# Decoder layer on one core: the norms' small products pinned inside block products, the first context loaded in 8 steps, constant products at the start, the last norm in pairs

## The chip, the cores and the metric

The kernel runs on one core of a Trainium2 chip. The time is device microseconds of one execution. Before the change it is 2510.47 us, the median of 3 runs (2509.59 to 2512.47). One execution was also profiled; all profile rows come from it.

## The reference

The program is one decoder layer in float32: 8 sequences of 100 tokens with 1024 features each, and a context of 722 tokens for each sequence. Three parts follow one another, each with a residual and a layer norm without weights:

```python
def _layernorm(x, axis=-1, eps=1e-05):
    m = jnp.mean(x, axis=axis, keepdims=True)
    v = jnp.var(x, axis=axis, keepdims=True)
    return (x - m) / jnp.sqrt(v + eps)
...
    # retention: 8 heads, keys of 128, values of 256, rotary embedding, decay mask
    scores = jnp.einsum('bihd,bjhd->bhij', q * scale, k) * D[None]
    o = jnp.einsum('bhij,bjhd->bihd', scores, v)
    rms = jax.lax.rsqrt(jnp.mean(o * o, axis=-1, keepdims=True) + EPS)
    o = o * rms * g_norm_weight
    o = o * (g * jax.nn.sigmoid(g))
    return o.reshape(B, T, H * DV) @ Wo
...
    # attention over context and own tokens: 16 query heads, 4 key heads of 128, RMS-normed q and k
    scores = jnp.einsum('blhd,bmhd->bhlm', q, k_full) * scale + mask
    probs = jax.nn.softmax(scores, axis=-1)
    out = jnp.einsum('bhlm,bmhd->blhd', probs, v_full)
    return out.reshape(B, L, NUM_HEADS * HEAD_DIM) @ wo
...
    # feed-forward, 4096 hidden
    return jnp.einsum('bsh,dh->bsd', jax.nn.silu(gate) * up, w_down)
...
x = _layernorm(x + _L0_attn_ref(x, ...))
x = _layernorm(x + _L0_xattn_ref(x, ctx_2048, ...))
x = _layernorm(x + _L0_ffn_ref(x, ...))
```

## The kernel before

Features lie on the 128 partitions, tokens along the free dimension. The 800 tokens are handled in two halves of N = 400 (4 sequences each). A vector of 1024 features is KT = 8 blocks of 128; QT = 4 is half of that.

**Products.** A float32 product is made of three fp32r matmuls: every operand is split in a high part (a cast on ScalarE, L67) and a low part (a subtraction on VectorE, L68), and `mm3` (L86 to L88) adds high x high, high x low and low x high in PSUM. One block product of 128 features over 1024 is `proj`: 8 k steps of 3 matmuls, 24 in all. An output projection (`out_proj`, called for both layer norms of the attention parts) has 2048 inputs, so a block takes 48 matmuls. PSUM has 3 banks under tag `a`, 4 under `s`, 1 under `v`.

**Weights** are loaded by `load_w`: a DMA of 512 KB on SP's queue into one of three `wst` tiles, and the split into one of four `w` tiles. Context tiles (`cs`, in `load_context`) use the same three `wst` tiles.

**Order of the work.** The program is traced in the order in which the code stands. A planner then orders each engine's instructions by priority (trace order) and by its own reckoning of when each is ready. Each engine works its own queue strictly in the planned order. `tc.keep_in_program_order` holds one instruction behind the one traced just before it on the same engine; before the change, only a few instructions are held so.

**Stages.** From the start to 430 us: retention (`w1`), mostly by a scheme of seven products in place of eight (`seven`). To 590 us: output projection and first norm (`out_proj` with `wo1`). To 850 us: queries, own keys and values (`w2`, the loop around L637), each with a rotary embedding (`rope`, L133 to L137), an RMS norm whose sum goes over the partitions on GpSimd (`all_red`, L125), and a store to DRAM (L654). In between lie `load_context(0)` (traced after the first four queries), and two early key products of the context. To 1610 us: attention of each sequence, with its context loaded one sequence at a time. To 1740 us: output projection and second norm (`wo2`). To 2450 us: feed-forward. The end is the last quarter of the down projection and the third norm (L995 to L1023).

**Norms.** The sum over features is a product with a constant matrix of 1/1024 (`onem`; `onem7` has 1/896): an F32 matmul, recorded as two instructions. The first half of each norm is handled by `norm_root`: the mean product (L279) after all eight blocks, 8 subtractions, squares and their sums (L260, L265), a variance product (L283), the inverse root (`inv_root`, L113 to L120), 8 scalings (L271). The second half is split in an early and a late part. `norm_early` takes the mean of the first seven blocks (six in the last norm) at L294, subtracts it (L297) and starts the variance (L299) while the last block is being computed. `norm_more` adds the last block's sum to `delta` (L305) and its squares to the variance (L306). `norm_late` corrects by delta: L312, L313, then 8 subtractions (L316), and scales. `s1` is the running sum of the blocks (L254); y is filled at L239, in the last norm at L1013 and L1014.

After the second norm `after2` (L795) mixes the two halves into the operands of the seven-product scheme.

Of the kernel before, what the change touches and what calls it, by code (L numbers as in the profile page):

```python
# [16 lines left out]
P = 128  # L17
# [17 lines left out]
NEG = -1.0e30  # L35
LN_EXP = "natural_log_exp_and_others"
# [3 lines left out]
def decoder_layer(ctx, tc, xT, cT, w1, wo1, w2, wo2, wc, w3, wd, gw, qw, kw, trig, dec, mask, out):  # L40
# [29 lines left out]
    def load_w(src, w=None, parts=1):  # L70
        st = wp.tile([P, KT * P], F32, tag="wst", name="wst", bufs=3)
        if w is None:
            w = wp.tile([P, 2, KT * P], FR, tag="w", name="w", bufs=4)
        for i in range(parts):
            c = slice(i * KT * P // parts, (i + 1) * KT * P // parts)
            nc.sync.dma_start(out=st[:, c], in_=src[:, c])
            split(w[:, :, c], st[:, c])
        return w
# [6 lines left out]
    def mm3(acc, lh, ll, rh, rl, start, stop, chain=False):  # L85
        nc.tensor.matmul(acc, lh, rh, start=start, stop=False, skip_group_check=chain)  # L86
        nc.tensor.matmul(acc, lh, rl, start=False, stop=False, skip_group_check=chain)  # L87
        nc.tensor.matmul(acc, ll, rh, start=False, stop=stop, skip_group_check=chain)  # L88

    def mmw(acc, w, k, rh, rl, start, stop):  # L90
        c = slice(k * P, (k + 1) * P)
        mm3(acc, w[:, 0, c], w[:, 1, c], rh, rl, start, stop)
# [7 lines left out]
    def proj(w, z, n=N, tag="a"):  # L100
        acc = bank(tag)[:, :n]
        for k in range(KT):
            t = z[k // QT]
            mmw(acc, w, k, t[:, 0, k % QT, :n], t[:, 1, k % QT, :n], k == 0, k == KT - 1)
        return acc
# [69 lines left out]

    def const(v, name):
        t = cp.tile([P, 1], F32, name=name)
        nc.vector.memset(t, v)
        return t
# [36 lines left out]
    def out_proj(half, w, load_o, res, yp, ybufs, p, make_z, dst, after=None):  # L216

        og = load_o(half)
        y = yp.tile([P, KT, N], F32, tag="y", name="y", bufs=ybufs)
        s1 = p.tile([P, N], F32, tag="s1", name="s1", bufs=2)  # L220
        first = 4 if half == 0 else 1
        for ms in [range(first)] + [[m] for m in range(first, KT)]:
            if half == 1 and KT - 1 in ms:
                early = norm_early(y, s1, p)
            accs = [bank(("aaasaaaa", "sssaaass")[half][m])[:, :N] for m in ms]
            for c in range(2):
                for m, acc in zip(ms, accs):
                    wt = load_w(w[m, c])
                    for k in range(KT):
                        kt = c * KT + k  # L230
                        rh, rl = og(kt)
                        a = acc if len(rh.shape) == 2 else bt(acc)
                        mmw(a, wt, k, rh, rl, kt == 0, kt == 2 * KT - 1)
            for m, acc in zip(ms, accs):
                rs = yp.tile([P, N], F32, tag="rs", name="rs", bufs=2)
                nc.sync.dma_start(out=rs, in_=res[half, :, m])
                if half == 1 and m == KT - 1:
                    nc.vector.tensor_tensor(rs, rs, early[0], ALU.subtract)
                nc.vector.tensor_tensor(y[:, m], acc, rs, ALU.add)  # L239
                if half == 0 or m < KT - 1:  # L240
                    add_up(s1, y, m)
        z = make_z(half)
        if half == 0:
            scaled(y, norm_root(y, s1, p), lambda m: dst[half, :, m], z)
        else:
            norm_more(y, early, p, KT - 1)
            norm_late(y, early, p, lambda m: dst[half, :, m], z)
        if after is not None:
            after(half, y)
        return z  # L250
# [25 lines left out]
    def norm_root(y, s1, p):  # L276
        n = y.shape[2]
        mean = bank("s")[:, :n]
        nc.tensor.matmul(mean, onem, s1, start=True, stop=True)  # L279
# [11 lines left out]
    def norm_early(y, s1, p, first=KT - 1):  # L291
        n = y.shape[2]
        mean = bank("s")[:, :n]
        nc.tensor.matmul(mean, onem7, s1, start=True, stop=True)  # L294
        f = (KT - 1) / first
        for m in range(first):
            nc.vector.scalar_tensor_tensor(y[:, m], mean, -f, y[:, m], ALU.mult, ALU.add)  # L297
        var, delta = bank("v")[:, :n], bank("s")[:, :n]
        nc.tensor.matmul(var, onem, squares(y, p, range(first)), start=True, stop=False, skip_group_check=True)  # L299
        return mean, var, f, delta, first  # L300

    def norm_more(y, early, p, m):

        _, var, _, delta, first = early
        nc.tensor.matmul(delta, onem, y[:, m], start=m == first, stop=m == KT - 1, skip_group_check=True)  # L305
        nc.tensor.matmul(var, onem, squares(y, p, [m]), start=False, stop=m == KT - 1, skip_group_check=True)  # L306

    def norm_late(y, early, p, dst, z=None):
        _, var, _, delta, _ = early
        n = y.shape[2]  # L310
        vs = p.tile([P, n], F32, tag="vs", name="vs")
        nc.scalar.activation(vs, delta, AF.Square)  # L312
        nc.vector.tensor_tensor(vs, var, vs, ALU.subtract)  # L313
        r = inv_root(p, vs, eps_ln, n)
        for m in range(KT):
            nc.vector.tensor_tensor(y[:, m], y[:, m], delta, ALU.subtract)  # L316
        scaled(y, r, dst, z)
# [104 lines left out]
    with sbuf("l1", 2) as p:  # L422
# [4 lines left out]
        for half in range(2):  # L427
            for j in (1, 2):
                zb["b%d%d" % (j, half + 1)] = big([P, 2, QT, N])
            if half == 0:  # L430
                w0 = load_w(w1[0, 0], parts=4)
            for k in range(KT):
                xs = temp()
                nc.sync.dma_start(out=xs, in_=xT[half, :, k])
# [89 lines left out]

        for i in range(2):
            for half in range(2):
                of_qk(half, i, proj((w0, wk0)[i], x[half]))
            mixed(i)
        for blk in range(2):
            w = load_w(w1[0, 2 + blk])  # L530
            for half in range(2):
                of_v(half, blk, proj(w, x[half]), True)
# [36 lines left out]
    z1p = z1pool.__enter__()  # L569
    with sbuf("ln1", 1) as p:  # L570
        z1 = [out_proj(half, wo1, load_o1, xT, p, 2, p, lambda _: [z1p.tile([P, 2, QT, N], FR, tag="z", name="z")
                                                                 for _ in range(2)], zd) for half in range(2)]
# [6 lines left out]
    def load_context(b):  # L579

        cz.clear()
        for hf in range(2):
            n = SN[hf]
            z = [big([P, 2, QT, SH]) for _ in range(2)]
            for k in range(0, KT, 2):
                cs = wp.tile([P, KT * P], F32, tag="wst", name="cs", bufs=3)
                cs = cs[:, :2 * n].rearrange("p (k n) -> p k n", k=2)
                nc.sync.dma_start(out=cs, in_=cT[b, :, k:k + 2, hf * SH:hf * SH + n])
                split(z[k // QT][:, :, k % QT:k % QT + 2, :n], cs)
            cz.append(z)  # L590
# [31 lines left out]
    early = []  # L622
    with sbuf("l2", 2) as p:
        for kv in range(NKV):
            for i0, i1 in ((0, 4), (4, 6)) if kv == 0 else ((0, 2), (2, 4), (4, 6)):
                if (kv, i0) == (0, 4):
                    load_context(0)
                ws = [load_w(w2[kv, i]) for i in range(i0, i1)]
# [5 lines left out]
                for half in range(2):  # L634
                    bs = slice(half * NB, (half + 1) * NB)
                    for i in range(i0, i1):
                        acc = proj(ws[i - i0], z1[half], tag=acc_tag())  # L637
# [157 lines left out]
    def after2(half, y):  # L795
        if half == 0:
            return
# [17 lines left out]

    with sbuf("lnp2", 1) as p:
        z2 = [out_proj(half, wo2, load_o2, zd, y2p, 1, p, make_z2, zd2, after2) for half in range(2)]
# [10 lines left out]
    ws = [[load_w(w3[i, part]) for part in range(2)] for i in range(2)]  # L828
    gs = {}
    for half in range(2):  # L830
        for i in range(2):
            ag, au = (proj(w, z2[half], tag=acc_tag()) for w in ws[i])
# [153 lines left out]

    for name in C:
# [9 lines left out]
    with sbuf("ln3", 2, "right") as lnp:  # L997
        ws = []
        for half in range(2):
            y = rows(half)  # L1000
            s1 = lnp.tile([P, N], F32, tag="s1", name="s1", bufs=2)
            early = None
            for m in range(KT):
# [5 lines left out]
                elif m == KT - 2:  # L1009
                    early = norm_early(y, s1, lnp, m)  # L1010
                acc = proj(ws[m], z3[half], tag=acc_tag())
                if early:
# [82 lines left out]
```

## Time and profile before

| | |
|---|---|
| median of the runs | 2510.47 us |
| profiled execution | 2510.48 us |
| its span, from first to last instruction | 2508.7 us |
| TensorE busy | 2461.3 us (98%) |
| VectorE busy | 1994.6 us (80%) |
| ScalarE busy | 1343.3 us (54%) |
| GpSimd busy | 478.8 us (19%) |
| mean DMA rate over the span | 173 GB/s |
| mean granted TensorE clock | 0.996 |

Times in rows are in us from the start of the span; a name such as L86 is the line of the kernel, and `a<-big,w` names the tile written and those read. Matmuls overlap at their ends, so the distance from one start to the next tells their pace: 0.18 us for 400 columns at full clock.

### The profile page before, as it was taken

How to read it: one execution, taken by the hardware profiler on the slowest of the kernel's cores; microseconds unless marked ns; L12 is line 12 of the kernel's file. 1: busy time of each engine (PE TensorE's matmuls, PEld its weight loads, DVE VectorE, ACT ScalarE, POOL GpSimd, SP SyncE). 2: the span in 40 equal slices, each digit the busy share in tenths (PEclk: the TensorE clock that was granted, in tenths of full speed). 3: DMA queues.
4: the chain of work that ended last, by engine and by line, in shares of the span. 5: the costliest groups of instructions: out<-in, count | busy, mean ns of one | idle time of the engine just before them, and what ended most of it. 6: DMA issues, size and time to landing. Idle time of an engine off the chain costs nothing.

```text
span 2508.7 us, 37154 instructions
## 1 busy us (share of the span) xinstructions
PE 2461.3 (98%) x14036; PEld 2438.4 (97%) x14036; DVE 1994.6 (80%) x3110; ACT 1343.3 (54%) x2264; POOL 478.8 (19%) x234
## 2 busy tenths in 40 slices
PE   8999999999899999999999999999999999999997
PEld 8999999999899999999999999999999999999997
DVE  7678877568999798999989998866987777666756
ACT  6667676335767565566666666533544444432221
POOL 0111111002555334433433434100000000000000
PEclk9999999999999999999999999999999999999999
DMA  7334445774444654554554563675455444389731
GB/s 241 111 111 127 137 142 185 237 270 146 150 148 132 213 175 143 173 173 142 168 186 133 174 195 116 209 253 162 137 178 196 166 169 162 121 297 329 259 100 53
DMA packets 224450, 433.96 MB, mean 173 GB/s; under 512 B 47338, under 2 KB 168042, under 8 KB 211854
## 3 DMA queue, kind: packets, MB, share of 16 engines
q1 hardware_dynamic: 223118, 427.39, 50.9%
q0 software_dynamic: 1152, 4.19, 1.1%
q8 instruction: 110, 1.80, 0.3%
q14 instruction: 70, 0.57, 0.1%
HBM read 322.18 MB, written 109.35 MB: 172 GB/s over the span
## 4 chain that ended last, share of the span: by engine, by line
PE 85%; DVE 9%; ACT 2%; issue 2%; DMA 2%; SPq 0%; DVEq 0%; ACTq 0%
PE a L88 17%; PE a L86 17%; PE a L87 17%; PE s L88 9%; PE s L87 9%; PE s L86 9%; PE v L87 1%; PE v L88 1%; PE v L86 1%; DVE r L120 1%; PE s L491 1%; PE s L688 1%; DVE r L119 1%; DVE w L68 1%; DVE t L650 1%
## 5 line engine op out<-in xcount | busy, mean ns | idle before, releaser
L86 PE MATMUL a<-big,w 128*128 128x400 f32 (+2 forms) x1808 | 610.5, 339 | 10.8 <-ACT big L67 7.3
L87 PE MATMUL a<-big,w 128*128 128x400 f32 (+2 forms) x1808 | 610.5, 338 | 0.0
L88 PE MATMUL a<-big,w 128*128 128x400 f32 (+2 forms) x1808 | 609.2, 338 | 0.0
L67 ACT CAST w<-wst 128x1024 fp32r<-128x1024 f32 (+1 forms) x231 | 239.4, 1038 | 389.9 <-PE a L88 134.9
L68 DVE TENSOR_TENSOR w<-wst,w 128x1024 fp32r<-128x1024 f32 (+1 forms) x231 | 282.9, 1226 | 119.2 <-ACT w L67 118.1
L86 PEld LDWEIGHTS a<-big,w 128*128 128x128 f32 x1808 | 341.1, 189 | 12.2 <-ACT big L67 7.3
L87 PEld LDWEIGHTS a<-big,w 128*128 128x128 f32 x1808 | 341.5, 189 | 1.3 <-DVE big L68 0.3
L88 PEld LDWEIGHTS a<-big,w 128*128 128x128 f32 x1808 | 341.5, 189 | 0.6
L86 PE MATMUL s<-big,w 128*128 128x400 f32 x664 | 230.6, 347 | 0.1
L88 PE MATMUL s<-big,w 128*128 128x400 f32 x664 | 229.0, 346 | 0.4 <-DVE w L68 0.4
L87 PE MATMUL s<-big,w 128*128 128x400 f32 x664 | 229.2, 345 | 0.0
L125 POOL PARTITION_ALL_REDUCE ss<-sq x56 | 160.5, 2871 | 332.9 <-DMA zd<-y 167.1
L605 POOL PARTITION_ALL_REDUCE kss<-ksq x64 | 171.9, 2686 | 121.9 <-ACT ksq L604 121.4
L86 PE MATMUL a<-z,w 128*128 128x400 f32 x488 | 169.6, 348 | 9.2 <-ACT r L118 5.6
L88 PE MATMUL a<-z,w 128*128 128x400 f32 x488 | 170.1, 349 | 0.7 <-DVE w L68 0.7
L87 PE MATMUL a<-z,w 128*128 128x400 f32 x488 | 170.0, 348 | 0.0
L87 PE MATMUL s<-z,w 128*128 128x400 f32 x400 | 138.1, 345 | 2.4 <-DVE z L68 2.4
L86 PE MATMUL s<-z,w 128*128 128x400 f32 x400 | 138.5, 347 | 0.0
L88 PE MATMUL s<-z,w 128*128 128x400 f32 x400 | 138.3, 346 | 0.0
L722 ACT ACTIVATE s<-s,rk 128x400 f32<-128x400 f32 x160 | 87.5, 591 | 90.9 <-DVE sm L742 65.3
L86 PEld LDWEIGHTS s<-big,w 128*128 128x128 f32 x664 | 124.6, 188 | 1.4 <-ACT w L67 0.4
L88 PEld LDWEIGHTS s<-big,w 128*128 128x128 f32 x664 | 125.1, 188 | 0.7 <-DVE w L68 0.7
(330 smaller groups left out, 5642.3 us busy)
## 6 DMA issues: line engine op xcount, KB each, us to landing
wst<-in_w SPq DMA_DIRECT2D x135, 512.0 KB
w<-wcd SPq DMA_DIRECT2D x64, 1024.0 KB
wst<-in_wo SPq DMA_DIRECT2D x64, 512.0 KB
hd<-h SPq DMA_DIRECT2D x12, 1400.0 KB
wst<-in_wd SPq DMA_DIRECT2D x64, 256.0 KB
big<-o1d SPq DMA_DIRECT2D x16, 800.0 KB
qd<-d SPq DMA_DIRECT2D x32, 400.0 KB
q<-qd SPq DMA_DIRECT2D x32, 400.0 KB
```

Of the source, the lines that this page charges most:

```text
L67: nc.scalar.copy(hi, src)
L68: nc.vector.tensor_tensor(lo, src, f32(hi), ALU.subtract)
L86: nc.tensor.matmul(acc, lh, rh, start=start, stop=False, skip_group_check=chain)
L87: nc.tensor.matmul(acc, lh, rl, start=False, stop=False, skip_group_check=chain)
L88: nc.tensor.matmul(acc, ll, rh, start=False, stop=stop, skip_group_check=chain)
L119: nc.vector.scalar_tensor_tensor(q, ss, eps, q, ALU.add, ALU.mult)
L120: nc.vector.scalar_tensor_tensor(q, q, 3.0, r, ALU.subtract, ALU.mult)
L125: nc.gpsimd.partition_all_reduce(y, x, P, op)
L491: nc.tensor.matmul(bt(o)[:, b], vv[:, b * P:(b + 1) * P], pf[:, b], start=True, stop=True)
L605: nc.gpsimd.partition_all_reduce(ss[:, at], sq[:, at], P, RED.add)
L650: nc.vector.scalar_tensor_tensor(t, t, -0.5 if i < 4 else -0.5 * math.sqrt(P), r, ALU.mult, ALU.mult)
L722: nc.scalar.activation(sc, sp, AF.Copy, scale=rk[:, c:c + 1])
```

## The change

Six things change.

1. `proj` and `out_proj` take a table `todo` of work to be traced ahead of a given k step. The products of a norm (mean, delta, variance) are traced and pinned there, inside the next block product: the means ahead of k step 4; delta ahead of step 4 and the variance ahead of step 7 of the first projection of the following stage. So the first projection with `w2[0,0]` and with `w3[0,0]` moves ahead of the late part of the norms.
2. The second halves' norm no longer scales the mean (`norm_early` only serves seven blocks), and in `norm_late` the 8 subtractions are pinned in order, 4 ahead of the variance's and 4 behind.
3. The first context is loaded in 8 steps, one after each of 8 projections of the first key head, each with its DMA pinned on SP's queue; before, all 8 were traced at once.
4. Weights for the first four queries, for the V blocks and for the first gate and up products are loaded at other places in the trace order; the very first weight comes by ScalarE's DMA queue and its split alternates with that of x.
5. 22 products of the constant matrix with itself stand at the start.
6. The last norm of the second half is a function of its own, `norm_last`, which subtracts and squares two blocks at a time (128 x 800).

```diff
+WARM = 22
...
+    def mm3(acc, lh, ll, rh, rl, start, stop, chain=False, pinned=False):
+        i = nc.tensor.matmul(acc, lh, rh, start=start, stop=False, skip_group_check=chain)
+        if pinned:
+            pin(i)
...
+    def proj(w, z, n=N, tag="a", todo=None):
         acc = bank(tag)[:, :n]
         for k in range(KT):
+            pinned = between(todo, k)
...
+    warm = bank("v")
+    for _ in range(WARM):
+        nc.tensor.matmul(warm[:, 0:P], onem, onem, start=True, stop=True)
...
             if half == 1 and KT - 1 in ms:
-                early = norm_early(y, s1, p)
-            accs = [bank(("aaasaaaa", "sssaaass")[half][m])[:, :N] for m in ms]
+                todo = {QT: lambda: early.update(norm_early(y, s1, p))}
...
         if half == 0:
-            scaled(y, norm_root(y, s1, p), lambda m: dst[half, :, m], z)
-        else:
-            norm_more(y, early, p, KT - 1)
-            norm_late(y, early, p, lambda m: dst[half, :, m], z)
+            return {QT: whole}, y
+        sq = squares(y, p, [KT - 1])
+        return {QT: lambda: summed(early["delta"], y[:, KT - 1], True, True),
+                KT - 1: lambda: (summed(early["var"], early["sq"], True), summed(early["var"], sq, False, True), late())}, y
+
+    def summed(acc, x, start=False, stop=False):
+
+        pin(nc.tensor.matmul(acc, onem, x, start=start, stop=stop, skip_group_check=True))
...
+        e["vs"] = p.tile([P, N], F32, tag="vs", name="vs")
+        nc.scalar.activation(e["vs"], e["delta"], AF.Square)
+        less(range(QT))
+        pin(nc.vector.tensor_tensor(e["vs"], e["var"], e["vs"], ALU.subtract))
+        less(range(QT, KT))
...
-                w0 = load_w(w1[0, 0], parts=4)
+                for i in range(QT):
+                    c = slice(2 * i * P, 2 * (i + 1) * P)
+                    nc.scalar.dma_start(out=st[:, c], in_=w1[0, 0][:, c])
...
+            wv.append(load_w(w1[0, 2 + i]))
             mixed(i)
         for blk in range(2):
-            w = load_w(w1[0, 2 + blk])
...
+        ws2 = [load_w(w2[0, 0])]
+        acc2 = [proj(ws2[0], z1[0], tag=acc_tag(), todo=todo)]
...
-                nc.sync.dma_start(out=cs, in_=cT[b, :, k:k + 2, hf * SH:hf * SH + n])
+                i = nc.sync.dma_start(out=cs, in_=cT[b, :, k:k + 2, hf * SH:hf * SH + n])
+                if pinned:
+                    pin(i)
...
-                if (kv, i0) == (0, 4):
-                    load_context(0)
...
+                        if kv == 0 and (half == 1 or i0 == 4):
+                            next(ctx0, None)
...
+    def norm_last(y, s1, p, dst):
+        first = KT - 2
+        pair = lambda i: y2[i][:, :, y.at]
+        wide = lambda ap: ap[:, None, :].to_broadcast([P, 2, N])
...
+        prods(0, range(QT))
+        pin(nc.tensor.matmul(mean, onem7, s1, start=True, stop=True))
+        prods(0, range(QT, KT))
+        f = (KT - 1) / first
+        sqs = []
+        for i in range(first // 2):
+            nc.vector.scalar_tensor_tensor(pair(i), wide(mean), -f, pair(i), ALU.mult, ALU.add)
+            sqs.append(p.tile([P, 2, N], F32, tag="sw", name="sw", bufs=3))
+            nc.scalar.activation(sqs[-1], pair(i), AF.Square)
+        pin(nc.vector.tensor_tensor(sqs[0], sqs[0], sqs[1], ALU.add))
+        q6 = add_block(0)
+        pin(nc.vector.tensor_tensor(sqs[0], sqs[0], sqs[2], ALU.add))
+        prods(1, range(KT))
+        q7 = add_block(1)
+        pin(nc.vector.tensor_tensor(sqs[1][:, 0], sqs[0][:, 0], sqs[0][:, 1], ALU.add))
+        summed(delta, y[:, KT - 2], start=True)
+        summed(var, q6, start=True)
+        summed(delta, y[:, KT - 1], stop=True)
+        summed(var, sqs[1][:, 0])
+        summed(var, q7, stop=True)
+        less = lambda i: pin(nc.vector.tensor_tensor(pair(i), pair(i), wide(delta), ALU.subtract))
+        less(0)
+        vs = p.tile([P, N], F32, tag="vs", name="vs")
+        nc.scalar.activation(vs, delta, AF.Square)
+        less(1)
+        pin(nc.vector.tensor_tensor(vs, var, vs, ALU.subtract))
+        less(2)
+        less(3)
+        scaled(y, inv_root(p, vs, eps_ln), dst)
```

## The prediction

> **What bounds the kernel now.** I read the page's head first, then the list of what TensorE waited for, then each engine's busy time in 10 us stretches where those waits lie, then single instructions at the start and the end.
>
> ```profile
> span 2508.7 us, 37154 instructions
> PE 2461.3 (98%) x14036; PEld 2438.4 (97%) x14036; DVE 1994.6 (80%) x3110; ACT 1343.3 (54%) x2264; POOL 478.8 (19%) x234
> ```
>
> TensorE is the bound: 2508.7 - 2461.3 = 47.4 us without a matmul, and of these some 19 us are the tail after the last block product. A change that leaves the products alone can win only from these 47 us and from matmuls run at half clock. Who holds TensorE up:
>
> ```profile
> PE a L86 <- ACT big L67: 7.3, 1, 7.3
> PE a L86 <- ACT r L118: 5.6, 1, 5.6
> PE a L86 <- ACT w L67: 4.2, 5, 1.3
> PE s L279 <- DVE s L254: 2.6, 2, 1.4
> PE s L87 <- DVE z L68: 2.4, 1, 2.4
> ```
>
> The columns are total us, times, longest. The first is the start. L279 is a norm's mean product, which stands directly behind the block product whose result it still has to wait for (at 510.9 us and 1659.2 us). The last is z1 of the second half, late at 605 us. The 5.6 us wait on "ACT r L118" is a PSUM bank not yet read out, at 629 us; what stands behind it shows in the stretches (columns: stretch, length, then busy us and count of PE, PEld, DVE, ACT, POOL):
>
> ```profile
> 600.00:610.00 10.00, 7.56 (x42) 7.23 (x41) 8.66 (x17) 7.63 (x16) 1.52 (x1) 1.00 0.86 308
> 630.00:640.00 10.00, 4.86 (x15) 4.85 (x16) 10.00 (x13) 6.27 (x13) 6.03 (x3) 0.70 0.37 139
> 650.00:660.00 10.00, 10.00 (x58) 9.94 (x57) 10.00 (x14) 7.76 (x15) 7.82 (x2) 1.00 0.42 130
> 720.00:730.00 10.00, 10.00 (x59) 10.00 (x58) 6.59 (x10) 6.76 (x13) 5.70 (x3) 1.00 0.63 196
> ```
>
> From 602 to 720 us VectorE is full and TensorE waits for it; at 720 us VectorE has caught up. In this stretch a TensorE gap that is closed is worth only what VectorE gains. Everywhere else TensorE's gaps count in full.
>
> **Part by part.**
>
> Means in the middle of a product, first halves (L279): the mean moves behind 4 of the next product's k steps, 12 matmuls x 0.18 us = 2.2 us. Its input is ready 1.4 us after the block's end (510.90 to 512.27), so the wait goes. The gap between matmul starts is 1.71 us at 510.56 and 1.62 us at 1658.83; less the 0.18 us of an ordinary step, -1.5 and -1.4 us. The mean itself, two F32 passes, costs the same wherever it stands. The last feed-forward norm has no such gap (0.64 us of DVE idle, no PE wait): 0.
>
> Second halves (L294, L299, L305, L306): before, the planner opens the next projection early and TensorE waits for its weights' cast, at 574.4 us and 1724.0 us, starts 1.47 us apart: 1.3 us each. The pinned order runs block 7 on with no hole. At 1724 VectorE is not full, so -1.3 us; at 574 it is, and I book that hole with the stretch below.
>
> The stretch from 574 to 720 us: the norm's instructions are the same in number: 7 subtracts, 7 sums of squares, 8 subtracts of delta, 8 scalings, 8 splits of 0.49 to 0.57 us on VectorE. What moves are the 8 context steps: each a 0.36 MB DMA on SP, a cast of 0.80 us on ScalarE and a split of 0.91 us on VectorE (7.1 us together), from ahead of z1's second half to behind its first projections. That lets z1 come about 7 us earlier, but VectorE must do the 7.1 us inside the full stretch instead. So the 2.4 and 5.6 us waits of TensorE are not the gain. The gain is VectorE's own idle time: 8.7 us from 574 to 720, of which 2.0 is the ordinary wait at block 6's end, and 1.08 + 1.93 us stand before context splits at 590 and 599. I take 2.5 us of these 3.0.
> Against it: each context DMA is now pinned behind what SP issued before it, which is a store of q that waits for VectorE, and weight loads stand behind both.
>
> ```profile
> 577.10 20.40 SPq L588 DMA_DIRECT2D cs<-in_cT  x8
> 633.99 13.92 SPq L654 DMA_DIRECT2D qd<-d  x4
> ```
>
> The first row is the burst of today, the second shows how long SP stands at stores in this stage. A context lands some 3.2 us after its issue (the chain shows 3.22, 3.20 and 3.17). If VectorE's order reckoned with it sooner, it waits up to 3.2 us, eight times: 25 us at worst; nothing if other work stands between. Bounds for the stretch: -7 (all idle beyond 2.0 recovered) to +25; taken -2.5, nearest to the idle that context splits have now.
>
> The start: 22 F32 products of the constant run first, before the inputs land. They replace nothing; they are to have the clock up.
>
> ```profile
> 7.30 0.70 PE L86 MATMUL a<-big,w 128*128 128x400 f32 x1 [7.30 <-ACT big L67]
> 12.41 0.54 PE L88 MATMUL a<-big,w 128*128 128x400 f32 x1
> 12.97 0.34 PE L87 MATMUL a<-big,w 128*128 128x400 f32 x1
> ```
>
> Until 12.8 us steps are 0.33 us, afterwards 0.18: half clock for 5.5 us from the first matmul. By this row: an F32 128-column product is two passes of 0.11 us at full clock (the transposes, 4 in 0.44 us), so 0.44 us at half clock. From the constants' memset (1.15 us) to 6.65 us 12.5 products pass, the other 9.5 take 2.1 us: inputs are first used at 8.8 us. The seventeenth real matmul then starts at 8.8 + 16 x 0.18 = 11.7 instead of 12.97: -1.3 us. The Trainium skill (TensorE: Matmul & The Clock Gate, Part 1: The HAM clock gate) says the clock rises after a busy window of about 3.4 us that runs free of the kernel: the rise then comes 3.4 to 6.8 us after the first product, and the gain is 2.4 to 0.7 us; the row's 5.5 lies inside.
> But the next hold-up, 1.28 us at 27.36, ends with a rope that stands on ScalarE behind casts of re-read x tiles, and these wait for DMA. The same skill's DMA: Bandwidth & Descriptors (Issuing engines are not separate DMA queues) speaks against w0's move to ScalarE's queue: all queues share the same 16 engines, only issue time is saved. This trace agrees that the engines are the limit:
>
> ```profile
> 8.00:12.00 4.00, 4.00 (x13) 3.96 (x13) 3.54 (x7) 2.90 (x6) 0.28 (x1) 1.00 0.99 353
> 24.00:28.00 4.00, 3.71 (x21) 3.37 (x19) 3.96 (x8) 3.86 (x7) 0.00 (x0) 1.00 0.91 343
> ```
>
> The last two columns are the DMA share and GB/s. By the rule, x and the weights land no sooner, and what TensorE gains by 12 us it can lose at 27; the two V weights, now ahead of the re-read tiles, put these 2 x 0.5 MB / 340 GB/s = 3 us later. Bounds +1.5 and -2.4; taken -0.7.
>
> The tail: the last product ends at 2489.70, the span at 2508.7: 19.0 us.
>
> ```profile
> 2485.37 2.98 DVE L297 SCALAR_TENSOR_TENSOR y<-s,y 128x400 f32<-128x400 f32 x6 [2.90 <-PE s L294]
> 2493.54 3.93 DVE L316 TENSOR_TENSOR y<-y,s 128x400 f32<-128x400 f32 x8
> 2497.39 0.56 DVE L313 TENSOR_TENSOR vs<-v,vs 128x400 f32<-128x400 f32 x1
> 2501.06 3.97 DVE L271 SCALAR_TENSOR_TENSOR y<-y,r 128x400 f32<-128x400 f32 x8
> ```
>
> The mean comes only with block 7 (L294 ended 2485.3), so squares and sums run until 2493.5, past the products. After the change it stands in the middle of block 6, some 2 us after that block's start at 2480: everything of blocks 0 to 5 is done under block 7. Then from the end of products: y7 added 0.7; its square to 1.2; five F32 sums of 0.85 us, the second delta ending at 2.6 and var at 4.3; the wide subtract (I price 128x800 at twice the 0.49 us step) two of them to 4.6, var minus delta squared to 5.2; Ln, Exp, Square 1.8; two more on VectorE 1.3; eight scalings 4.0; the last store 3.65 (2505.03 to 2508.7): 15.9 instead of 19.0, -3.1 us. The other two subtracts lie under ScalarE's 1.8 us. If that cover is gone, they cost 2 us. One thing is late here: VectorE scales the first half from 2477.4 to 2481.4 just as block 5 must be added for the mean; up to +1.
>
> Sum: -0.7 - 1.5 - 2.5 - 1.4 - 1.3 - 3.1 = -10.5 us. The profiled execution took 2510.48 us, the span and 1.8 us around it, and equals the median of the runs, 2510.47. So **2500.0 us**. The stages from 850 to 1650 and from 1780 to 2450 us have next to no TensorE gap and I cost them at 0.
>
> **The rivals.**
>
> Slower: the pinned contexts. If VectorE, whose queue is in order, stands at each context split for the landing less one instruction of 0.5 us, 2.7 us x 8 = 21.6 us, in a stage where it is the bound: -10.5 + 21.6 = +11, 2521. For it: SP's long stands at stores. Against: other ready work of 0.5 to 2 us pieces is plentiful there. It decides from 15.5 / 8 = 1.9 us a step on.
>
> Nothing: the same wait at half that size. With 1.1 us a step the stretch costs 9 us, and the start yields nothing: -10.5 + 0.7 + 9 = -1, 2509. The norms' gaps are then closed and given back.
>
> More: VectorE's backlog shrinks so far that the half-clock windows go too (634 to 641, 678 to 682, 702 to 706 us) and all 6.7 us of its idle time is won: another 4 us, with 1.7 more at the start: 2494.
>
> **How the numbers follow.** Main case 0.55, own range 2495 to 2505; more 0.14; nothing 0.13; slower 0.18. A difference of 0.2%, 5 us, is about what a measurement here can tell from none. Faster 0.55 + 0.14 = 0.69, same 0.13, slower 0.18. The range 2490 to 2514 leaves out most of the slower case (0.13) and 0.04 below.
>
> **What would show it.** No wait of L279 on "DVE s L254"; block 7 of both attention norms without a hole; mean of the last norm inside block 6 and a tail near 16 us; z1's wait at 605 gone, but VectorE still full from 600 to 700. First real matmul near 8.8 us at 0.18 us steps, and a hold-up near 28 us as long as or longer than now. I am wrong if VectorE shows waits on "cs" beyond 5 us in all, or TensorE new waits on weight casts in the query stage, or if the start loses.

## The result and the profile after

After the change the kernel takes 2541.59 us (median; 2539.63 to 2543.07) against 2511.06 us before, measured beside it: a ratio of 1.0121, 95% interval 1.0109 to 1.0133. It is 30.5 us slower. The prediction said 2500 us, with 2490 to 2514 as its range.

The head of the page and the list of TensorE's waits after the change (total us, times, longest):

```profile
span 2541.2 us, 37210 instructions
PE 2467.3 (97%) x14080; PEld 2445.5 (96%) x14080; DVE 1994.6 (78%) x3101; ACT 1345.4 (53%) x2261; POOL 473.8 (19%) x234
...
PE s L87 <- ACT w L68: 46.4, 3, 31.8
...
PE s L1069 <- DVE s L287: 2.0, 1, 2.0
PE a L87 <- ACT big L68: 2.0, 1, 2.0
PE s L87 <- DMA big<-o1d: 1.4, 1, 1.4
```

TensorE's work grew by 6 us, VectorE's not at all, the span by 32.5 us. Of the old waits, the first (7.3 us), the two on "DVE s L254" and the 5.6 us on a PSUM bank are gone. In their place stand three waits for the cast of a weight, 46.4 us together. To find the stage, I take the time at which each stage ends, in four profiles (before in us from its start, the others as a difference to it; the third and fourth are experiments told below). A stage or block ends here with VectorE's last instruction on its results, so stages overlap; the last block product ends with its last matmul:

| end of | before | after | context at once | own tiles |
|---|---|---|---|---|
| retention | 427.4 | -0.4 | -1.3 | +0.1 |
| block 0 of norm 1, first half | 473.7 | +1.0 | -0.6 | +1.9 |
| block 6 of norm 1, second half | 575.3 | +0.2 | -1.1 | +1.3 |
| block 7 of it | 586.5 | -1.2 | -2.2 | -0.1 |
| query stage | 854.4 | +31.6 | 0.0 | -0.1 |
| attention | 1639.8 | +33.1 | +1.0 | +1.4 |
| block 6 of norm 2, second half | 1724.9 | +34.1 | +3.4 | +3.9 |
| block 7 of it | 1736.3 | +32.7 | +2.0 | +2.5 |
| last block product | 2489.7 | +35.6 | +4.9 | +5.4 |
| the span | 2508.7 | +32.5 | +1.8 | +2.3 |

Everything is lost between 586 and 854 us: 32.8 us. The waits lie there, at 620.84 us (32.16 us from one matmul's start to the next) and at 677.72 us (13.22 us). Each engine's busy time in these stretches after the change (stretch, length, then busy us and count of PE, PEld, DVE, ACT, POOL, granted clock, DMA share, GB/s):

```profile
620.80:653.00 32.20, 0.39 (x3) 0.05 (x1) 27.47 (x43) 19.04 (x35) 11.56 (x4) 0.57 0.50 165
653.00:677.70 24.70, 21.92 (x103) 20.94 (x104) 10.28 (x14) 9.20 (x16) 4.75 (x2) 0.85 0.28 86
677.70:691.00 13.30, 0.49 (x4) 0.07 (x2) 5.67 (x10) 5.24 (x8) 0.76 (x1) 0.50 0.51 168
```

TensorE does three matmuls in 32 us. VectorE works through the queries that stand in PSUM meanwhile, then runs dry itself. The sums of its stretches from 574 to 720 us, after and then before:

```profile
sum 146.00, PE 98.59 PEld 95.60 DVE 105.34 ACT 77.98 POOL 42.55; mean PE 24.65 PEld 23.90 DVE 26.34 ACT 19.49 POOL 10.64
```

```profile
sum 146.00, PE 131.04 PEld 127.06 DVE 139.22 ACT 98.32 POOL 61.27; mean PE 32.76 PEld 31.77 DVE 34.80 ACT 24.58 POOL 15.32
```

VectorE is idle for 40.7 us of them, before for 6.8. The transfer engines are half free (DMA share 0.50 and 0.51 in the two waits), so this is no lack of bandwidth. What the weight waited for is in SP's own row of issues (start, us, what):

```profile
615.90 15.29 SPq L702 DMA_DIRECT2D qd<-d  x4
631.24 0.43 SPq L625 DMA_DIRECT2D cs<-in_cT  x1
...
645.48 0.32 SPq L702 DMA_DIRECT2D qd<-d  x1
645.89 0.39 SPq L625 DMA_DIRECT2D cs<-in_cT  x1
646.37 1.08 SPq L75 DMA_DIRECT2D wst<-in_w  x2
...
684.36 0.43 SPq L625 DMA_DIRECT2D cs<-in_cT  x1
684.84 14.92 SPq L75 DMA_DIRECT2D wst<-in_w  x7
```

Store of a query (`qd<-d`), context step, store, context step: the two weights with which the next projections begin (`w2[0,4]`, `w2[0,5]`) are issued at 646.37 us, 25 us after TensorE had gone idle. The chain that ended last shows the rest of the way in its order:

```profile
646.37 5.51 DMA wst<-in_w
651.90 1.05 ACT w L68
652.98 1.24 DVE w L69
654.26 0.70 PE s L91
```

The stores wait for VectorE. In the list of SP's waits from 574 to 720 us:

```profile
SPq L702 <- DVE d L69: 63.3, 10, 17.8
```

The idle time also took the clock. The granted clock is half from 625.41 to 659.54 us and from 676.61 to 697.09 us; of this, 653 to 659.5 and 691 to 697 us fall on real work and cost half their length, 6.4 us. The two steps (45.0 us beyond ordinary ones), these 6.4 and a new wait for a value cast (2.6) make 54.0; the old waits from 600 to 720 us (5.6, 2.4, 1.9, 1.9, 1.3 and 0.7, together 13.8) and the old stretches at half clock (6.8, 3.4 and 3.4 us, half of which is 6.8) are gone: 33.4, close to the 32.8 measured.

### The profile page after: what moved, and what is told of

It reads as the page before. It is cut to its first block, busy times and chain, and to the rows that moved or that the text cites. A ratio compares the mean times of both kernels' runs of the same rounds, so it can differ in the third digit from the quotient of the medians.

```text
span 2541.2 us, 37210 instructions
## 1 busy us (share of the span) xinstructions
PE 2467.3 (97%) x14080; PEld 2445.5 (96%) x14080; DVE 1994.6 (78%) x3101; ACT 1345.4 (53%) x2261; POOL 473.8 (19%) x234
## 4 chain that ended last, share of the span: by engine, by line
PE 91%; DVE 4%; DMA 3%; ACT 1%; issue 1%; SPq 0%; DVEq 0%; ACTq 0%
PE a L91 18%; PE a L87 18%; PE a L90 18%; PE s L91 10%; PE s L87 10%; PE s L90 10%; PE v L90 2%; PE v L91 2%; PE v L87 2%; PE s L522 1%; PE s L736 1%; DMA wst<-in_w 1%; DVE r L131 1%; PE s L159 1%; DVE y L304 0%
## 5 line engine op out<-in xcount | busy, mean ns | idle before, releaser
L87 PE MATMUL s<-z,w 128*128 128x400 f32 x400 | 141.6, 354 | 44.6 <-ACT w L68 44.6
L91 PE MATMUL a<-z,w 128*128 128x400 f32 x488 | 168.6, 345 | 0.0
L90 PE MATMUL a<-z,w 128*128 128x400 f32 x488 | 168.3, 345 | 0.0
L87 PE MATMUL a<-z,w 128*128 128x400 f32 x488 | 167.5, 343 | 0.5 <-ACT w L68 0.5
L90 PE MATMUL s<-z,w 128*128 128x400 f32 x400 | 140.3, 351 | 0.0
L91 PE MATMUL s<-z,w 128*128 128x400 f32 x400 | 140.0, 350 | 0.2 <-DVE w L69 0.2
```

The costliest lines, as they stand in the source:

```text
L87: i = nc.tensor.matmul(acc, lh, rh, start=start, stop=False, skip_group_check=chain)
```

## The experiments

Two theories for the two waits. **The queue**: a weight stands on SP behind pinned context DMAs, and these behind stores that wait for VectorE. **The tile**: a context step holds one of the three `wst` tiles, and the next weight gets its tile only behind it. And a rival from the prediction: VectorE itself stands at the context splits.

**The pin alone taken away.** The kernel after, with

```diff
-    ctx0 = context_steps(0, True)
+    ctx0 = context_steps(0)
```

> The changed kernel with the eight context DMAs not pinned; everything else as changed. Theory (weights): the two waits of TensorE of 32.0 us at 621 us and 13.0 us at 678 us on weight casts come from weight loads that stand on SP's queue behind pinned context DMAs, which stand behind stores of q that wait for VectorE. Without the pin both waits go; VectorE is still full there, so about 10 us of waits on it come back as before the change: 2500 to 2512 us. Rival (VectorE waits at context splits, as priced in the prediction): the splits are still spread over the same eight products, so VectorE's idle of 42 us between 574 and 720 us stays largely: over 2530 us. Rival (moved projections and single weight loads are at fault, not the contexts): over 2530 us.

Measured: 2519.35 us, ratio to before 1.0025 (1.0017 to 1.0032). Both waits are gone and 22 us come back, but 7 us fewer than the least that this theory expected. What remains is in TensorE's list of waits from 574 to 860 us in this kernel:

```profile
PE a L87 <- ACT d L68: 7.6, 1, 7.6
PE s L159 <- ACT vt L156: 5.3, 3, 3.1
PE a L87 <- DVE t L146: 3.5, 2, 2.4
```

These are of the old kind: the first and third are PSUM banks not read out, the second is a value block (`vt`) not yet copied out of PSUM. So the pin is needed for the damage, but without it the query stage still ends 6.2 us late.

**The context at once, as before.** The kernel after, with

```diff
-    ctx0 = context_steps(0, True)
...
+                if (kv, i0) == (0, 4):
+                    load_context(0)
...
-                        if kv == 0 and (half == 1 or i0 == 4):
-                            next(ctx0, None)
```

> The changed kernel with the first context loaded at once where the kernel before has it, ahead of the group of key and value products; no steps, no pin. Theory (weights): as without the pin, 2498 to 2512 us, a little less or more by the place of the 7.1 us of context splits on VectorE. Rival (moved projections and single weight loads): over 2530 us, since these are kept.

Measured: 2511.91 us, ratio 0.9997 (0.9988 to 1.0005). The whole loss is in the context's part of the change, and all the rest of it together is worth nothing that can be measured. That is the second finding, and the third column of the table says where: the stage ends swing between -2.2 and +4.9 us.

**The steps alone.** The kernel before, with the 8 pinned steps and nothing else:

```diff
-    def load_context(b):
+    def context_steps(b, pinned=False):
...
+                if pinned:
+                    tc.keep_in_program_order(i)
...
+                        if kv == 0 and (half == 1 or i0 == 4):
+                            next(ctx0, None)
```

> The kernel before with only the context's eight pinned steps of the change. Theory (weights): the same two waits appear, 25 to 40 us over before: 2536 to 2551 us. Rival (moved projections and single weight loads): within 5 us of before, 2506 to 2516 us.

Measured: 2545.24 us, ratio 1.0123 (1.0093 to 1.0154): the loss of the whole change, from one part of it. TensorE waits twice for the cast of a weight from 600 to 720 us, 43.6 us together.

**Context tiles of their own.** The kernel after, pin and steps as they are, but

```diff
-                cs = wp.tile([P, KT * P], F32, tag="wst", name="cs", bufs=3)
+                if pinned:
+                    cs = ka.tile([P, 2 * SH], F32, bufs=1, tag="cvt", name="cs")
+                else:
+                    cs = wp.tile([P, KT * P], F32, tag="wst", name="cs", bufs=3)
```

> The changed kernel, context steps pinned as in it, but the context tiles of these steps take a buffer of their own (that of the context values, free at that time) in place of one of the three that the weights use. Theory (weights wait for a buffer that a pinned context tile holds): the weights are issued early and the 32 and 13 us waits go, with the pins still there: 2498 to 2515 us. Rival (the pin's place on SP's queue alone, whatever the buffers): near the changed kernel, 2535 us or more.

Measured: 2510.08 us, ratio 0.9996 (0.9989 to 1.0003). With the pin and the stores still there, the loss is gone: 31.5 us between the two kernels. SP's issues in this kernel:

```profile
614.34 12.49 SPq L75 DMA_DIRECT2D wst<-in_w  x4
626.99 12.03 SPq L705 DMA_DIRECT2D qd<-d  x4
639.07 0.43 SPq L628 DMA_DIRECT2D cs<-in_cT  x1
```

Once they need no tile that a context step holds, the weights are issued at 614.34 us, ahead of the stores.

**The steps on another queue.** The kernel after, tiles shared, with

```diff
-                i = nc.sync.dma_start(out=cs, in_=cT[b, :, k:k + 2, hf * SH:hf * SH + n])
                 if pinned:
-                    pin(i)
+                    pin(nc.scalar.dma_start(out=cs, in_=cT[b, :, k:k + 2, hf * SH:hf * SH + n]))
```

> The kernel after, with the 8 pinned context DMAs issued on ScalarE's queue in place of SP's; the shared tiles stay, and the pin now stands behind the ScalarE instruction traced before. Theory 1 (the tile decides: a context step that stands pinned late holds one of three tiles that the next weights are planned behind, wherever it is issued): the waits for the cast of w at 621 and 678 us stay, about 20 to 32 us lost, 2530 to 2545 us. Theory 2 (SP's queue decides: the weights stand behind the stores of q that SP waits at): the waits go, 2508 to 2516 us.

Measured: 2536.87 us, ratio 1.0094 (1.0079 to 1.0108). The loss stays, 4.7 us smaller. SP's issues in this kernel:

```profile
615.97 26.44 SPq L703 DMA_DIRECT2D qd<-d  x6
642.50 2.74 SPq L75 DMA_DIRECT2D wst<-in_w  x2
646.37 3.37 SPq L703 DMA_DIRECT2D qd<-d  x2
```

No context DMA is left on SP, and the weights still stand behind six stores of q, issued 3.9 us sooner than after the change. So the first theory falls as a cause by itself: the loss needs the shared tile, not context DMAs on SP. How the tile acts is read from the rows and the code, not tried apart. In the code the two weights come behind four context steps that take tiles of the same three, so the planner puts them late in SP's order, and there the stores of q stand ahead of them. SP itself waits for no tile at that point: in both kernels it issues the first of the two weights within 0.1 us of the end of the issue ahead of it.

**Own tiles, no pin.**

```diff
-                if pinned:
+                if b == 0:
                     cs = ka.tile([P, 2 * SH], F32, bufs=1, tag="cvt", name="cs")
...
-    ctx0 = context_steps(0, True)
+    ctx0 = context_steps(0)
```

> The kernel after, with the context tiles of the 8 steps in a buffer of their own and their DMAs not pinned. It completes a square: pinned or not, shared tiles or own. Theory (only the two together hold the weights back; neither alone does): no weight load waits in the query stage, between 2508 and 2513 us, as with own tiles and the pin (2510.1). Rival (the steps without the pin lose on their own, as the 2519.4 us of the kernel with shared tiles and no pin could mean, because the planner places them where VectorE is full): 2516 to 2521 us.

Measured: 2512.71 us, ratio 1.0005 (0.9996 to 1.0015). The square is complete (medians, us; before 2511):

| the 8 steps | tiles shared with the weights | tiles of their own |
|---|---|---|
| pinned | 2541.59 | 2510.08 |
| not pinned | 2519.35 | 2512.71 |

Neither the pin nor the steps cost anything with own tiles; with shared tiles the steps cost 8 us and the pin 22 more.

**Less work for VectorE in the full stretch.** The prediction took VectorE for the bound from 602 to 720 us. The kernel before, with ScalarE writing a plain copy as the low part of q and k. It leaves out the subtraction that makes the low part, and with it 23 us of VectorE's work in the query stage (ScalarE writes these 40 tiles instead, 0.52 us each):

```diff
-                        split2(d[:, :, 0], d[:, :, 1], bt(t))
+                        nc.scalar.copy(d[:, :, 0], bt(t))
+                        nc.scalar.copy(d[:, :, 1], bt(t))
```

> The kernel before with the low parts of the query and key tiles in the query stage written by ScalarE as a plain copy instead of VectorE's subtraction; the low part of q and k is thereby wrong, and a subtraction of 0.57 us for each of 40 tiles is left out on VectorE. Theory (VectorE sets the pace from 602 to 720 us, so that a norm that comes sooner wins nothing there): 23 us less for VectorE, TensorE's waits in that stage (some 16 us, and the half clock after them) go in great part: 2497 to 2503 us. Rival (the pace is set by SP's queue or by GpSimd's sums): 2508 us or more.

Measured: 2505.18 us, ratio 0.9976 (0.9968 to 0.9984): 6 us for 23 us of work, between what the theory and the rival expected. The same two stretches, first of this kernel:

```profile
600.00:720.00 120.00, 109.06 (x580) 106.86 (x579) 111.20 (x151) 94.49 (x186) 61.69 (x21) 0.96 0.46 156
720.00:850.00 130.00, 127.55 (x712) 127.02 (x711) 106.64 (x149) 97.42 (x194) 63.75 (x28) 0.99 0.48 162
```

and then of the kernel before:

```profile
600.00:720.00 120.00, 106.17 (x554) 103.69 (x552) 116.64 (x166) 85.05 (x165) 61.27 (x21) 0.94 0.44 144
720.00:850.00 130.00, 126.94 (x712) 125.63 (x711) 114.20 (x166) 88.35 (x172) 68.62 (x27) 1.00 0.51 167
```

TensorE has 3.5 us more done by 850 us. VectorE, with 15 instructions fewer in the first stretch, is idle for more of it (8.8 in place of 3.4 us). VectorE at full was a bound in part. What the rest is was not told apart.

**The first halves' means alone.** The kernel before, with only these norms traced and pinned inside the next block:

```diff
-        nc.tensor.matmul(mean, onem, s1, start=True, stop=True)
+        pin(nc.tensor.matmul(mean, onem, s1, start=True, stop=True))
...
+                        pinned = bool(todo) and kt == QT
+                        if pinned:
+                            todo.pop()()
...
-            scaled(y, norm_root(y, s1, p), lambda m: dst[half, :, m], z)
+            todo.append(whole)
```

> The kernel before with only the first halves' mean (and with it the first halves' norm) of the two attention norms moved into the middle of the next block product, pinned there. Prediction as made: the waits of 1.5 and 1.4 us at 511 and 1659 us go and nothing comes in their place: -2.9 us, 2508.4 beside 2511.3 us. Theory now (given back at once): at 519 us TensorE waits some 1.4 us for the second half's o1 tiles, and at 1668 us some 2.0 us for a weight cast that stands on ScalarE behind the norm's squares, with a half-clock window after it: 0 to +1 us, 2511 to 2512 us.

Measured: 2511.6 us, ratio 1.0003 (0.9995 to 1.0011). The waits on "DVE s" at the mean are gone, as in the kernel after, and nothing is gained. From the chain of this kernel at the second norm:

```profile
1662.72 0.69 PE s L291 x2
...
1663.42 3.94 DVE y L293 x8
1667.36 0.50 DVE s L277
...
1668.32 0.52 ACT sq L272
1668.84 0.94 ACT w L67
...
1670.43 0.33 PE s L91
```

The mean now comes some 2 us after the block's end, in the middle of the next, and so do the eight subtractions behind it. ScalarE takes its instructions in order; the next weight's cast (L67) stands behind squares that wait for the sums, and TensorE waits for that cast: a step of 2.17 us from one matmul to the next, with a clock at half for 3.4 us behind it (0.33 us a matmul). The kernel after shows the same place:

```profile
1695.52 3.94 DVE y L314 x8
...
1700.94 0.94 ACT w L68
```

At the first norm the wait closed at 511 us came back in the kernel after at 518 us, where the next operand tile was not there:

```profile
508.90 10.59 DMA big<-o1d
...
519.63 0.42 PE s L87
```

SP issues these loads when it did before, whatever the norm does; before the change, then after:

```profile
506.59 2.97 SPq L565 DMA_DIRECT2D big<-o1d  x4
```

```profile
506.73 2.98 SPq L597 DMA_DIRECT2D big<-o1d  x4
```

TensorE came to that operand sooner and stood for it. The matmul that waits, the 37th of the second half, starts at 519.63 us; before the change it started at 519.55 us, without a wait.

**The last norm alone.** The kernel before with `norm_last`, its mean behind the whole of block 6 in place of its middle:

```diff
+        prods(0, range(KT))
+        pin(nc.tensor.matmul(mean, onem7, s1, start=True, stop=True))
...
-            else:
-                norm_late(y, early, lnp, dst)
+        norm_last(y, s1, lnp, dst)
```

> The kernel before with only the last norm of the second half as in the change (in pairs, five sums behind the products), its mean behind block 6. Theory: the tail after the last product shrinks from 19.0 to 15.9 us and nothing waits for the mean: -3.1 us, 2508.2 us beside 2511.3 for the kernel before. Rival (late squares take the place of the late mean): the tail stays over 18 us, 2510 us or more.

Measured: 2510.0 us, ratio 0.9995 (0.9987 to 1.0003). The tail is 17.8 us (2490.43 to 2508.2), so 1.2 us shorter than before, not 3.1. With the mean this late, VectorE begins the pairs at 2486.10 us, and adds block 7 only 2.1 us after the last product:

```profile
2486.10 2.79 DVE L1024 SCALAR_TENSOR_TENSOR y<-s,y 128x800 f32<-128x800 f32 x3 [2.90 <-PE s L1020]
...
2492.50 0.57 DVE L1014 TENSOR_TENSOR y<-y,a 128x400 f32<-128x400 f32 x1
```

**The start alone.** The kernel before with the 22 constant products, the first weight by ScalarE's queue and the V weights earlier:

```diff
+    warm = bank("v")
+    for _ in range(22):
+        nc.tensor.matmul(warm[:, 0:P], onem, onem, start=True, stop=True)
...
+                    nc.scalar.dma_start(out=st[:, c], in_=w1[0, 0][:, c])
...
+            wv.append(load_w(w1[0, 2 + i]))
```

> The kernel before with only the start of the change: 22 constant products first, the first weight by ScalarE's queue with its split between those of x, the V weights ahead of the re-read x tiles. Prediction as made: -0.7 us (bounds -2.4 and +1.5), 2510.6 us. Rival (the first block products run at full clock into inputs that land no sooner, and the wait may drop the clock again): the retention stage ends 0 to 0.5 us sooner, within 0.5 us of before.

Measured: 2511.74 us, ratio 1.0003 (0.9995 to 1.0011). Retention ends 1.1 us sooner; at block 7 of the first norm it is 0.4 us later than before, at the end of the query stage 3.2 us later.

**Two versions that mend more.** First, own tiles, both weights of the second half's first block traced ahead of the norm, and the last mean behind block 6:

```diff
+            pre = [load_w(w[ms[0], c]) for c in range(2)] if todo and half == 1 else []
...
-                    wt = load_w(w[m, c])
+                    wt = pre[c] if pre else load_w(w[m, c])
...
-        prods(0, range(QT))
+        prods(0, range(KT))
```

> The changed kernel with three amendments: context steps with a buffer of their own (as in the run before); both weights of the first block of a second half are traced ahead of the norm that is put inside that block; the last norm's mean stands behind block 6 and not in its middle. Theory (order on ScalarE and SP, not the norms' place, eats the gains): the 2.0 us wait for a weight cast behind the norm's squares at 1668 us goes and with it a half-clock window (2.4 us together), and the 2.0 us wait for s1 at 2485 us goes: 2510.1 - 4.4 = 2505.7 us. Rival (these gaps are filled by other waits): 2509 to 2512 us.

Measured: 2509.78 us, ratio 0.999 (0.9984 to 0.9997). It is the one version with all its computation whose interval lies below 1, by 1.6 us; with twelve versions compared, that can be chance. The wait for the weight's cast at the second norm stayed (1.8 us); the wait at the last mean went, but the tail is 17.5 us.

Second, own tiles without the pin and every mean as late as its inputs seemed to ask, at k step 12 of 16 in the attention norms and ahead of step 7 in the last:

```diff
-                        pinned = between(todo, k) if c == 0 and m == ms[0] else False
+                        pinned = between(todo, k) if c == (0 if m == KT - 1 else 1) and m == ms[0] else False
...
-        prods(0, range(QT))
+        prods(0, range(KT - 1))
```

> The changed kernel with context tiles of their own and no pin, the first halves' norms one weight later (ahead of k step 12 of 16 in the block in place of 4), and the last norm's mean ahead of k step 7 in place of 4. Theory (order costs can be mended one by one): no wait behind squares at 1668 us (-2.4 against the run with own tiles and pins), the wait for the last norm's mean down from 2.0 to 0.4 us with the tail at 16 to 17 us (-1), w<-wcd no longer behind pinned contexts: 2504 to 2508 us. Rival (each gap closed opens another): 2509 to 2512 us.

Measured: 2517.08 us, ratio 1.0024 (1.0016 to 1.0032), a miss. The list of TensorE's waits in this kernel names new ones:

```profile
PE s L87 <- DMA big<-o2d: 4.4, 2, 2.8
PE s L87 <- DMA big<-o1d: 3.0, 4, 1.1
```

The later norms ran into the loads of the attention outputs, 7.4 us together. Another 4.0 us are lost in the query stage, which ends 5.0 us later than before when block 7 of the first norm ended 1.0 us later; what costs them was not tried apart.

## Why the prediction was wrong

**The stretch from 574 to 720 us** is the step that failed. It said that "weight loads stand behind both" the context DMAs and the stores, and then priced only what VectorE would wait for a context's landing (bounds -7 to +25, taken -2.5). It put TensorE's wait for a weight at nothing. Measured: +32.8 us to the end of the query stage, outside even the upper bound, and on TensorE. The size of the missing wait is not a landing of 3.2 us but the time until the last store ahead of it: 621 to 646 us, plus 5.5 us of landing and 1.05 us of cast. The row was shown ("633.99 13.92 SPq L654", four stores of q): it said how long SP stands at stores where no weight was urgent. The idle time that the gain started from, 8.7 us, is 6.8 us by the busy time of the stretches. I also did not count the tiles: context and weights share three, so a context step that is held late holds a weight late. The square above shows that this sharing, together with the pin, is the cause.

**The slower rival** had the right part of the change, the pinned contexts, and the wrong carrier. VectorE did wait for the casts of contexts (14.3 us in all from 574 to 720 us, beyond the 5 us that I named as the sign), but it waited in a stage that TensorE already held up: with the context DMAs on ScalarE's queue these waits of VectorE are 7.8 us, and the loss is still some 26 us. The other sign, new waits of TensorE for weight casts in the query stage, is what came.

**VectorE as the bound there** was right in part: 23 us less of its work gave 6 us.

**The start**, -0.7: hardly clear of noise, and gone afterwards. In the nine kernels with this start retention ends between 1.8 us sooner and 0.3 us later than before, 0.7 us sooner on the mean; in the four experiments that leave retention as it was it ends between 0.8 us sooner and 0.6 us later. Inputs were first used at 7.47 us, not 8.8, since the clock rose at 4.18, 3.1 us after the first product. The 3.4 to 6.8 us for this was an estimate from the window in the Trainium skill (TensorE: Matmul & The Clock Gate, Part 1: The HAM clock gate), and 3.1 lies below it. It also said that TensorE could lose the time again at 27 us; that hold-up is gone, and another one came at 12 us, 2.32 us long, where the next x tile was not cast. By the first block of norm 1 nothing is left (+1.0, -0.6, +1.9).

**The means**, -1.5 and -1.4: the two waits went as told, and came back at 518 us (1.73 us step, operand tile late) and at 1700 us (2.17 us, weight's cast late). The term that I left out is what TensorE needs next. At the first norm that is an operand load that keeps its old time: 1.5 us sooner at the operand is 1.4 us longer at its load. At the second norm it is a cast behind the norm's subtractions and the squares on ScalarE, and these moved with the norm.

**The hole before block 7**, -1.3 each: right. Between block 6 and block 7 the kernel after wins 1.4 us at both norms (+0.2 to -1.2, and +34.1 to +32.7).

**The tail**: predicted 19.0 to 15.9, measured 2525.33 to 2541.2, 15.9 us. The sum of VectorE's steps was right; a 128x800 step took 0.93 to 0.99 us, twice 0.49 as priced. But "up to +1" for the late mean was 2.0. VectorE's row in the kernel after:

```profile
2511.74 3.97 DVE L304 SCALAR_TENSOR_TENSOR y<-y,r 128x400 f32<-128x400 f32 x8
2515.62 0.57 DVE L287 TENSOR_TENSOR s<-s,y 128x400 f32<-128x400 f32 x1
2516.11 0.57 DVE L1121 TENSOR_TENSOR y<-y,a 128x400 f32<-128x400 f32 x1
2516.59 1.18 DVE L287 TENSOR_TENSOR s<-s,y 128x400 f32<-128x400 f32 x2
2518.80 2.79 DVE L1074 SCALAR_TENSOR_TENSOR y<-s,y 128x800 f32<-128x800 f32 x3 [1.03 <-PE s L1069]
```

The eight scalings of the first half stand ahead of the sums that the mean needs, and the mean is pinned ahead of the rest of block 6. So TensorE waits 2.0 us; from block 7 of norm 2 to the last product all three versions of the table lose 2.9 us, and the tail's 3.1 us are paid for: -0.2 in all.

**The stages costed at 0**: attention lost 1.0 to 1.5 us in the three versions of the table. A wait at its start grew (from 1.7 us to between 2.6 and 2.8, for the cast `cvt`); whether that is all of it was not tried.

What stays open: why the unpinned steps with shared tiles still cost 8 us. The square says that the shared tiles are needed for it. It is not a late weight as with the pin: TensorE waits for no cast of a weight by ScalarE in that kernel's query stage, and its longest wait, 7.6 us, is for a PSUM bank. What in the planned order makes it so was not told apart.

## What to carry to other kernels

Before a DMA is held in its place, list what shares its destination tiles and what is planned behind it on its queue; the price is the wait of the last of these for the slowest thing ahead of it, not the landing of the DMA itself. A tile of its own, 2.9 KB per partition in a buffer that stood unused at that time, made the same edit free. And a wait that is closed is won only when the next thing in the chain is ready as well: here the gaps closed at the start, at both means and in the tail, 0.7 to 3 us each, were given back at an operand, a cast or a mean that was not ready any sooner.

## What the runs showed of the hardware

**The clock.** The full stretches between changes of the granted clock are multiples of one length in all of these profiles, within the reading: 3.41, 6.83, 10.24, 17.07, 20.48, 34.13 us. The clock rose between 3.1 and 5.3 us after the first constant product in the nine kernels with this start, and between 4.1 and 6.4 us after the first matmul in the five without it. The Trainium skill (TensorE: Matmul & The Clock Gate, Part 1: The HAM clock gate) has a free-running window of about 3.4 us; the scatter agrees, and the earliest rise lies below one full window. A step of 2.32 us between two matmuls at 12 us was enough to take the clock to half after the change, and one of 2.17 us at 1668 us in the kernel with the means alone too. One of 2.17 us at 1700 us after the change was not, and neither was one of 3.14 us at 1666 us in the last of the versions above: at this size the length alone does not decide. The same page (Why this matters for your kernels) warns of idle time beyond some 3 us; here less did it.

**VectorE beside GpSimd.** A scaling that takes 0.57 us took 2.11 us in the kernel after while GpSimd summed over the partitions, as VectorE's row shows, and GpSimd's beside it:

```profile
712.56 2.11 DVE L698 SCALAR_TENSOR_TENSOR t<-t,r 128x400 f32<-128x400 f32 x1
```

```profile
712.12 2.98 POOL L136 PARTITION_ALL_REDUCE ss<-sq  x1 [1.54 <-ACT sq L693]
```

It is not one case. Of the 40 such scalings of queries and keys in this kernel, the 15 that met no sum of GpSimd took 0.58 us at most, and of the 25 that overlapped one, 12 took 1.4 to 2.1 us. Part of VectorE's busy time in the query stage is thus not its own work. What makes it wait there was not tried.
